# Seven block products in the first steps of three LSTMs, with their input sums made one LSTM earlier

## Chip, cores and metric

The kernel runs on one core of a Trainium2 chip. The metric is the device time of one execution in microseconds (us), the median of three executions. The core has a tensor engine for matrix products (PE; its weight loads are a queue of their own, PEld), a vector engine (DVE), a scalar engine for activation functions (ACT), GpSimd (POOL) and a queue, SP, that issues transfers.

## The reference

Four layers follow each other on x of 128 batches x 64 tokens x 256 channels: a two-matrix graph convolution with batch norms, a graph network with LSTMs, and two attention layers. Each normalises x over the channels, takes the positive part and adds its result to x. The change touches the second layer alone. It is, in the reference's words:

```
h = relu(einsum('ts,bsh->bth', adj, x @ Wg0 + bg0))
h = relu(einsum('ts,bsh->bth', adj, h @ Wg1 + bg1))
for p in range(1, 5):
    nw = Tv // p
    wins = h[:, :nw * p, :].reshape(Bv * nw, p, Hd)
    last = _lstm_last(Wih[p-1], Whh[p-1], bih[p-1], bhh[p-1], wins)
    idx = arange(nw) * p + (p - 1)
    h = h.at[:, idx, :].set(last.reshape(Bv, nw, Hd))

step(h, c):   g = x_t @ Wih.T + h @ Whh.T + bias;   i, f, gg, o = split(g, 4)
              c = sigmoid(f) * c + sigmoid(i) * tanh(gg);   h = sigmoid(o) * tanh(c)
```

So four LSTMs of one, two, three and four tokens run one after the other, each on what the one before has written. The states h and c are zero at the first step: that step needs only the products with Wih, of only three gates (i, g and o).

## The kernel before, in words

Everything is 32-bit float. The 8192 tokens lie in 16 chunks of 512 columns. The LSTM stage (about 274 to 1526 us of the profile) takes the chunks in eight pairs. A pair's tokens stand in one tile hT, channels on the partitions: two channel halves c (or k, as the operand of a product) of 1024 columns each, 64 tokens x 16 batches. For each pair the generator `lstms` (L1384) runs `single` (L1278, the one-token LSTM) and then `lstm` (L1026) for p = 2, 3 and 4. An LSTM of p tokens works on n = 512, 336 or 256 windows; m is half of n: 256, 168 or 128. `halves` splits the columns in two, j = 0 and 1.

All products of 256 x 256 by 256 x n that are not first steps, and all of `single`, are already done in seven block products of half the columns, in place of eight. `differences` (L309) makes four sums of the four operand blocks (t1 = b12 - b11, t3 = b22 - b12, t2 = b22 - t1, t4 = b21 - t2). A block product is called by its kind, 1 to 7: kinds 1, 2 and 3 take blocks b11, b21 and b22 as they are, kinds 5, 6, 7 and 4 take t1, t2, t3 and t4. `BLOCKS` (L1024) gives the index of each kind's weight block in a weight set, for Wih and Whh. Weight sets (one for each p and gate) are made in the first layer by `weight_sums` (L744), written to memory, and brought back into six buffers by `load_sets` (L883), two to four at a time, from the SP queue. A set has 15 blocks, 960 KB.

The first step of `lstm` before the change (L1107 to L1137) does not use block products: twelve whole products (three gates x two output halves x two operand halves, L1125) of n columns accumulate in six PSUM banks. Six of them need only operand half 0; a `yield` stands after these six. ACT then takes each bank through its activation (`first_acts`, L1112), DVE multiplies i by g (L1118), ACT takes tanh (L1119), DVE makes the state h (`new_state`, L1077) and, for the next step's products, its sums dh (L313 to L316). Behind the twelve products PE runs six block products of the next step that need no state (`A`, L1197), and then yields again. `operands_x` (L1086) makes the sums of the inputs of a later step, on POOL; the ones for step 1 stand at the beginning of `lstm`. For p = 3, where the number of windows is odd, three more POOL copies (L1097) bring blocks 1, 2 and 3 into contiguous columns.

Each later step (L1199 to L1256) does the same for the gates with both weights (class `Unit`): ACT copies two of the block products out of PSUM (L1160), DVE adds the others to them (L1163), ACT applies the activations (L1068).

The order is written out by hand: within this stage PE, DVE, ACT, POOL and SP each keep the order in which the program issues their instructions. Other work is put between: the loop at L1512 counts the `yield`s n of one pair, 0 to 21 (0 to 3 in `single`, 4 to 7 for p = 2, 8 to 13 for p = 3, 14 to 21 for p = 4), and at each one it issues the units that the lists at L1448 to L1456 name. They are parts of the convolutions of the next pairs (CONV and BEGUN, FIRST and BEGUN_FIRST in the first pair), the return of finished pairs (RESIDUAL) and the start of the next layer (AHEAD, LATE; FINAL in the last pair). Units that matter below, by number within `convolutions` (L980): unit 2 is `ln_stats` (DVE statistics L159, L160, then two POOL instructions for 1/sqrt, L99 and L100), unit 3 is a small DVE product that reads the POOL result (L194) and half of the normalisation on ACT (L196), unit 4 the other half, unit 5 an aggregation on PE (L214), unit 6 its two DVE copies (L1005), unit 7 a product (L915), unit 8 its lower bound on DVE (L921), unit 9 a product (L929), unit 10 its DVE add (L935). A unit of RESIDUAL adds transposed squares on DVE (L284).

PSUM has eight banks in this stage: two each with the tags x, y, z, and two for the units.

Of the kernel before, what the change touches and what calls it, by code (L numbers as in the profile page):

```python
# [13 lines left out]
P = 128  # L14
# [5 lines left out]
def kernel(  # L20
# [666 lines left out]
    with tc.manual_schedule(engines={mybir.EngineType.PE}):  # L687
# [56 lines left out]
        def weight_sums(p, q):  # L744
# [10 lines left out]
            far = dram.tile([P, 15, P], F32, tag=f"ws{p}{q}", name=f"wfar_{p}_{q}", bufs=1)  # L755
            nc.sync.dma_start(far[:, :9], w[:, :9])
            nc.sync.dma_start(far[:, 9:], w[:, 10:])
# [125 lines left out]
    def load_sets(n):  # L883
        for _ in range(min(n, len(coming))):
            p, q = coming.pop(0)
            wsets[p, q] = w1.tile([P, 15, P], F32, tag="wset", name=f"wset_{p}_{q}", bufs=6)
            nc.sync.dma_start(wsets[p, q], wfar[p, q])
# [136 lines left out]
    BLOCKS = {1: (0, 8), 2: (2, 9), 3: (7, 14), 4: (3, 10), 5: (4, 11), 6: (5, 12), 7: (6, 13)}  # L1024

    def lstm(p, hv, name, follows):  # L1026


        nb = hv.shape[3]
        nw = hv.shape[2] // p  # L1030
# [4 lines left out]
        inner = nb // 2 if odd else nb  # L1035
# [3 lines left out]

        def tokens(k, s, j):  # L1040
            v = hv[:, k, cols(s), :]
            if odd:
                return v[:, :, j * inner : (j + 1) * inner]
            return v[:, j * nw // 2 : (j + 1) * nw // 2, :]
# [41 lines left out]
        def operands_x(s):  # L1086

            t = l1.tile([P, 7 * (T // 3) * NB], F32, tag="xd", name=f"xd_{name}_{s}", bufs=2)
            t = [folded(t[:, i * m : (i + 1) * m]) for i in range(7 if odd else 4)]
            b = {(k, j): tokens(k, s, j) for k in range(KD) for j in range(2)}  # L1090
            for f in differences(nc.gpsimd, t[:4], b[0, 0], b[0, 1], b[1, 0], b[1, 1]):
                f()
            o = dict(zip((5, 6, 7, 4), t))
            for i, (kind, kj) in enumerate(((1, (0, 0)), (2, (1, 0)), (3, (1, 1)))):
                if odd:

                    nc.gpsimd.tensor_copy(t[4 + i], b[kj])  # L1097
                o[kind] = t[4 + i] if odd else b[kj]
            return o

# [4 lines left out]
        ox = {1: operands_x(1)}  # L1105

        banks = {(q, c): bank(f"g{q}_{name}_{c}", tag) for q, tag in ((0, "y"), (2, "z"), (3, "x"))  # L1107
                 for c in range(KD)}
        def first_acts(*qs):
            for q in qs:  # L1110
                for c in range(KD):
                    nc.scalar.activation(  # L1112
                        columns_of(gate(q, c)),
                        natural(banks[q, c][:, :n].rearrange("p (w b) -> p w b", b=nb)),
                        AF.Tanh if q == 2 else AF.Sigmoid, bias=bs[:, q * KD + c : q * KD + c + 1])
# [5 lines left out]
        products = [(q, c, k) for k in range(KD) for q in GATES[:3] for c in range(KD)]  # L1121
        for at, (q, c, k) in enumerate(products):
            if at == 6:
                yield
            nc.tensor.matmul(  # L1125
                banks[q, c][:, :n].rearrange("p (w b) -> p w b", b=nb), wsets[p, q][:, 2 * k + c, :],
                hv[:, k, : (nw - 1) * p + 1 : p, :], start=(k == 0), stop=(k == KD - 1))
        first_acts(0, 2)
        first_cell(0)
        first_acts(3)  # L1130
        first_cell(1)
        for c in range(KD):
            new_state(0, c, every)
            if not c:
                dh[0]()
# [63 lines left out]
        for s in range(1, p):  # L1199
            last = s == p - 1  # L1200
            B = [Unit(q, s) for q in (1, 3)]
            if not last:
                ox[s + 1] = operands_x(s + 1)
# [74 lines left out]
    def single(b, name, begun):  # L1278
# [57 lines left out]
        if begun:  # L1336
            for f in first + rest:
                f()
# [713 lines left out]
```

## Time and profile before

| | us |
|---|---|
| median of 3 executions | 1901.11 (1900.84 to 1902.15) |
| the profiled execution | 1899.42 |
| its span, first to last instruction | 1897.3 |
| PE busy | 1862.9 (98%) |
| DVE, ACT, POOL busy | 1238.9, 1015.9, 569.7 (65, 54, 30%) |
| LSTM stage from the first L1125, 293.5 to 1490 us: PE, DVE, ACT, POOL busy | 1180.9, 753.5, 652.8, 289.0 of 1196.5 |
| one pair of chunks, 611.0 to 768.5 us: PE, DVE, ACT, POOL busy | 155.9, 102.3, 86.8, 39.0 of 157.5 |

"Busy" is the time in which at least one instruction of the engine runs. PE records each 32-bit product as two instructions, so that the twelve products of a first step appear as 24. A group in the page's part 5 has its busy time, the mean duration of one, and the idle time of the engine just before it with what ended it. Matmuls overlap: the distance between the starts of two is shorter than the duration of one. In the timeline, each line has a start, a duration, the engine, the line of the program, what is written from what, and in brackets the idle time before it.

The pairs of chunks 2 to 7 run alike: from the first L1125 of p = 2 to the first product with a state, each takes 17.61 us; for p = 3 it is 11.49 to 11.64 us, and for p = 4 9.97 us. The first pair takes 16.99, 12.87 and 10.06 us, the last one 13.33, 9.68 and 9.01 us.

### The profile page before, as it was taken

The page shows a single profiled execution, that of the slowest core. Times are in us where ns is not written, and L with a number is a line of the kernel's source. Part 1 is how long each engine was busy: PE and PEld are TensorE (multiplying, and loading weights), DVE is VectorE, ACT ScalarE, POOL GpSimd, SP SyncE. Part 2 cuts the span into 40 slices and gives each one's busy share as a digit, 9 for nine tenths or more (in the row PEclk, how much of TensorE's full clock was granted, in tenths as well). Part 3 has the DMA queues.
Part 4 walks back from the last instruction along what each step waited for, and adds up shares of the span by engine and source line. Part 5 has one row for each costly group of instructions (what it writes and reads, how often), then busy time and mean ns, then how long its engine had stood idle before and what let it go on. Part 6 is the DMA issues. An engine that isn't in the chain of part 4 may idle for free.

```text
span 1897.3 us, 39092 instructions
## 1 busy us (share of the span) xinstructions
PE 1862.9 (98%) x15077; PEld 1478.2 (78%) x15077; DVE 1238.9 (65%) x3150; ACT 1015.9 (54%) x2284; POOL 569.7 (30%) x752
## 2 busy tenths in 40 slices
PE   8999989999999999999999999999999999999998
PEld 6877856895896798689589679868969967777776
DVE  6768746566576666667657666665565567677776
ACT  5766544556456446555645645655565544444453
POOL 5856621212221322222322231222122213233232
PEclk9999999999999999999999999999999999999999
DMA  3223643225334433333433443333144345444433
GB/s 114 78 68 149 232 168 109 72 88 184 106 129 145 144 128 129 113 119 115 150 117 129 150 139 137 130 109 106 54 150 139 103 134 157 135 139 152 143 114 113
DMA packets 111273, 241.45 MB, mean 127 GB/s; under 512 B 11504, under 2 KB 74864, under 8 KB 111088
## 3 DMA queue, kind: packets, MB, share of 16 engines
q1 hardware_dynamic: 110192, 237.09, 37.1%
q8 instruction: 119, 1.95, 0.4%
q0 software_dynamic: 320, 1.05, 0.2%
q10 hardware_dynamic: 576, 0.82, 0.1%
q14 instruction: 66, 0.54, 0.1%
HBM read 170.50 MB, written 68.42 MB: 126 GB/s over the span
## 4 chain that ended last, share of the span: by engine, by line
PE 86%; DVE 7%; POOL 3%; ACT 2%; issue 1%; DMA 0%; DVEq 0%; SPq 0%; ACTq 0%
PE x L1154 22%; PE z L1154 11%; PE g L1125 7%; PE v L1542 6%; PE y L1154 5%; PE x L1308 4%; PE y L1308 3%; PE p_q L1549 3%; PE v L915 3%; PE X L1738 3%; PE X L423 2%; PE X L499 2%; PE u L929 2%; PE Y L1738 1%; PE Y L423 1%
## 5 line engine op out<-in xcount | busy, mean ns | idle before, releaser
L1163 DVE TENSOR_TENSOR gates<-gates,x 128x128 f32<-128x128 f32 (+2 forms) x384 | 118.3, 320 | 332.1 <-PE x L1154 324.9
L1154 PE MATMUL x<-xd,wset 128*128 128x128 f32 (+2 forms) x1280 | 285.6, 311 | 0.7 <-DVE gates L1163 0.2
L1154 PE MATMUL x<-hd,wset 128*128 128x128 f32 (+2 forms) x1152 | 246.7, 303 | 0.0
L1212 POOL TENSOR_TENSOR gates<-gates 128x512 f32<-128x512 f32 (+2 forms) x48 | 74.9, 1560 | 521.7 <-ACT gates L1068 521.7
L1154 PEld LDWEIGHTS x<-xd,wset 128*128 128x128 f32 x1280 | 202.1, 190 | 19.1 <-DVE gates L1163 6.1
L1068 ACT ACTIVATE gates<-gates,bias 128x256 f32<-128x256 f32 (+4 forms) x384 | 170.4, 490 | 56.2 <-DVE gates L1163 52.8
L1154 PEld LDWEIGHTS x<-hd,wset 128*128 128x128 f32 x1152 | 185.1, 191 | 5.0
L1125 PE MATMUL g<-hT,wset 128*128 128x256 f32 (+2 forms) x576 | 183.9, 474 | 1.1 <-DVE hT L1079 1.1
L1160 ACT COPY gates<-y 128x128 f32<-128x128 f32 (+2 forms) x192 | 54.2, 293 | 212.9 <-PE y L1154 212.4
L1125 PEld LDWEIGHTS g<-hT,wset 128*128 128x128 f32 x576 | 108.6, 190 | 69.7 <-issue 38.5
L1154 PE MATMUL z<-hs,wset 128*128 128x128 f32 (+2 forms) x768 | 154.0, 303 | 0.0
L1154 PEld LDWEIGHTS z<-hs,wset 128*128 128x128 f32 x768 | 119.8, 191 | 3.3
L1160 ACT COPY gates<-x 128x128 f32<-128x128 f32 (+2 forms) x192 | 56.4, 295 | 93.7 <-PE x L1154 92.9
L1163 DVE TENSOR_TENSOR gates<-gates,z 128x128 f32<-128x128 f32 (+2 forms) x384 | 104.3, 315 | 0.1
L1068 ACT ACTIVATE gates<-x,bias 128x128 f32<-128x128 f32 (+2 forms) x192 | 74.7, 389 | 49.4 <-PE x L1154 46.5
L1154 PE MATMUL z<-hT,wset 128*128 128x128 f32 (+1 forms) x512 | 97.1, 302 | 0.0
L1112 ACT ACTIVATE gates<-g,bias 128x512 f32<-128x512 f32 (+2 forms) x144 | 74.5, 559 | 32.1 <-PE g L1125 31.6
L1154 PE MATMUL x<-hs,wset 128*128 128x128 f32 (+2 forms) x384 | 84.8, 303 | 0.0
L1223 ACT ACTIVATE gates<-cell 128x256 f32<-128x256 f32 (+2 forms) x144 | 55.2, 384 | 50.5 <-DVE cell L1222 49.0
L1154 PE MATMUL y<-xd,wset 128*128 128x128 f32 (+2 forms) x384 | 77.4, 304 | 3.4 <-ACT gates L1112 3.4
L1154 PE MATMUL y<-hd,wset 128*128 128x128 f32 (+2 forms) x384 | 80.1, 311 | 0.0
L1154 PEld LDWEIGHTS z<-hT,wset 128*128 128x128 f32 x512 | 76.7, 191 | 3.9 <-ACT gates L1112 0.6
(329 smaller groups left out, 4211.5 us busy)
## 6 DMA issues: line engine op xcount, KB each, us to landing
wset<-wfar SPq DMA_DIRECT2D x96, 960.0 KB, 6.6
hT<-far_h SPq DMA_DIRECT2D x124, 128.0 KB, 3.1
far_h<-hm SPq DMA_DIRECT2D x16, 512.0 KB, 3.0
far_n<-xs SPq DMA_DIRECT2D x16, 512.0 KB, 3.3
xs<-far_n SPq DMA_DIRECT2D x64, 128.0 KB, 4.2
far_x<-xs SPq DMA_DIRECT2D x16, 512.0 KB, 3.0
x<-far_x SPq DMA_DIRECT2D x64, 128.0 KB, 3.2
xt<-in_x_dram SPq DMA_DIRECT2D x15, 512.0 KB, 4.1
```

Of the source, the lines that this page charges most:

```text
L423: nc.tensor.matmul(self.banks[tag][:, i * CH // 2 : (i + 1) * CH // 2], w, self.at[kind], start=first and not i, stop=True, skip_group_che ...
L915: nc.tensor.matmul(banks[m], wg0_sb[:, k, m * P : (m + 1) * P], agg[:, k, :], start=(k == 0), stop=(k == KD - 1))
L1068: nc.scalar.activation(gate(q, c, part), src, AF.Tanh if q == 2 else AF.Sigmoid, bias=bs[:, q * KD + c : q * KD + c + 1])
L1112: nc.scalar.activation(columns_of(gate(q, c)), natural(banks[q, c][:, :n].rearrange("p (w b) -> p w b", b=nb)), AF.Tanh if q == 2 else AF. ...
L1125: nc.tensor.matmul(banks[q, c][:, :n].rearrange("p (w b) -> p w b", b=nb), wsets[p, q][:, 2 * k + c, :], hv[:, k, : (nw - 1) * p + 1 : p, ...
L1154: nc.tensor.matmul(folded(self.psum(kind)), wsets[p, self.q][:, BLOCKS[kind][i], :], (ox[self.s] if part == "x" else oh)[kind], start=firs ...
L1160: nc.scalar.copy(gate(self.q, kind // 5, halves[kind // 5]), self.psum(kind))
L1163: nc.vector.tensor_add(gate(self.q, *dst), gate(self.q, *a), self.psum(kind))
L1212: nc.gpsimd.tensor_mul(gates[:, 0, :, :n], gates[:, 0, :, :n], gates[:, 2, :, :n])
L1308: nc.tensor.matmul(folded(ps(g, kind)), wih1[:, g, KINDS1[kind], :], right[kind], start=kind in (2, 5, 1), stop=True, skip_group_check=True)
L1542: nc.tensor.matmul(ps[:, i, :], hT[:, k, j, :], w[:, k, first : first + D], start=(k == 0), stop=(k == KD - 1))
L1738: nc.tensor.matmul(st[c, tag][:, i * CH // 2 : (i + 1) * CH // 2].rearrange("p (a n) -> p a n", n=P), w, st[c, "o7"][kind], start=first an ...
```

## The change

1. The first step of p = 2, 3 and 4 is done in seven block products for each of the three gates (class `First`): 21 products of m columns in place of 12 of n. ACT copies kinds 1 and 5 of each gate, the `yield` follows, then kinds 3, 2, 6, 7 and 4 with DVE adds for 2, 6, 3 and 7, activations and cell products in between. Kinds 1, 6, 7 and 4 of a gate accumulate in the same columns of one bank.
2. `operands_x` is called by a new function `ending` at the end of the preceding LSTM, for steps 0 and 1: eight POOL sums there in place of four at the beginning of `lstm`. For p = 3 the three copies are gone, and the products read the strided blocks. The same is done for the sums of `single` (`block_sums`), which move ahead of the last `yield` of the p = 4 LSTM. The buffers for the sums are three of 1024 columns in place of two of 1176.
3. The weight sets have 14 blocks, 896 KB: block 1 was used by the old first step alone. Each set is written to memory in three transfers in place of two.
4. Three units move one `yield` later: CONV unit 4 of the second chunk (4 to 5), BEGUN unit 2 of the first (14 to 15), AHEAD unit 5 of the first (15 to 16). The six products of `A` stand in the order of kinds 3, 2, 5, before 5, 3, 2.

The diff, cut to its core:

```diff
@@ weight_sums
-            far = dram.tile([P, 15, P], F32, tag=f"ws{p}{q}", name=f"wfar_{p}_{q}", bufs=1)
-            nc.sync.dma_start(far[:, :9], w[:, :9])
-            nc.sync.dma_start(far[:, 9:], w[:, 10:])
+            far = dram.tile([P, 14, P], F32, tag=f"ws{p}{q}", name=f"wfar_{p}_{q}", bufs=1)
+            for at, n, src in ((0, 1, 0), (1, 7, 2), (8, 6, 10)):
+                nc.sync.dma_start(far[:, at : at + n], w[:, src : src + n])
@@ load_sets
-            wsets[p, q] = w1.tile([P, 15, P], F32, tag="wset", name=f"wset_{p}_{q}", bufs=6)
+            wsets[p, q] = w1.tile([P, 14, P], F32, tag="wset", name=f"wset_{p}_{q}", bufs=6)
@@ before lstm
+    def operands_x(p, hv, name, s):
+        nw, nb, inner, tokens = columns_x(p, hv)
+        m = nw * nb // 2
+        t = l1.tile([P, 2 * CH], F32, tag="xd", name=f"xd_{name}_{s}", bufs=3)
+        t = [t[:, i * m : (i + 1) * m].rearrange("p (a b) -> p a b", b=inner) for i in range(4)]
+        b = {(k, j): tokens(k, s, j) for k in range(KD) for j in range(2)}
+        for f in differences(nc.gpsimd, t, b[0, 0], b[0, 1], b[1, 0], b[1, 1]):
+            f()
+        return {5: t[0], 6: t[1], 7: t[2], 4: t[3], 1: b[0, 0], 2: b[1, 0], 3: b[1, 1]}
@@ lstm
-        ox = {1: operands_x(1)}
-        products = [(q, c, k) for k in range(KD) for q in GATES[:3] for c in range(KD)]
-        for at, (q, c, k) in enumerate(products):
-            if at == 6:
-                yield
-            nc.tensor.matmul(
-                banks[q, c][:, :n].rearrange("p (w b) -> p w b", b=nb), wsets[p, q][:, 2 * k + c, :],
-                hv[:, k, : (nw - 1) * p + 1 : p, :], start=(k == 0), stop=(k == KD - 1))
-        first_acts(0, 2)
+        class First:
+            def __init__(self, q, tags):
+                self.q, self.ps = q, [bank(f"{t}{q}_{name}_{i}", t) for i, t in enumerate(tags)]
+            def psum(self, kind):
+                return self.ps[kind in (2, 3)][:, m:n] if kind in (5, 3) else self.ps[kind in (2, 3)][:, :m]
+            def product(self, kind):
+                nc.tensor.matmul(folded(self.psum(kind)), wsets[p, self.q][:, BLOCKS[kind][0], :], ox[0][kind],
+                                 start=kind in (1, 3), stop=True, skip_group_check=True)
+            def copy(self, c, j, kind):
+                nc.scalar.copy(gate(self.q, c, halves[j]), self.psum(kind))
+            def add(self, dst, a, kind):
+                nc.vector.tensor_add(gate(self.q, dst[0], halves[dst[1]]),
+                                     gate(self.q, a[0], halves[a[1]]), self.psum(kind))
+        firsts = [First(q, tags) for q, tags in ((0, "yz"), (2, "yz"), (3, "xx"))]
+        all_first(1, lambda u: u.copy(0, 0, 1))
+        all_first(5, lambda u: u.copy(1, 1, 5))
+        yield
+        all_first(3)
+        all_first(2, lambda u: u.add((0, 0), (0, 0), 2))
+        all_first(6, lambda u: u.add((0, 1), (1, 1), 6), lambda u: u.add((0, 1), (0, 1), 3),
+                  lambda u: act(u.q, 0, every, gate(u.q, 0)))
         first_cell(0)
-        first_acts(3)
+        all_first(7, lambda u: u.add((1, 1), (1, 1), 7), lambda u: act(u.q, 1, halves[1], gate(u.q, 1, halves[1])))
+        new_state(0, 0, every)
+        dh[0]()
+        all_first(4, lambda u: act(u.q, 1, halves[0], u.psum(4)))
         first_cell(1)
-        for c in range(KD):
-            new_state(0, c, every)
-            if not c:
-                dh[0]()
+        new_state(0, 1, every)
         dh[1]()
         dh[2]()
@@ lstm
-        each(A, pe(5, "x"), pe(3, "x"), pe(2, "x"))
+        each(A, pe(3, "x"), pe(2, "x"), pe(5, "x"))
...
             if last:
                 load_sets(2)
+                ending()
@@ lstms
+        def ending(p):
+            if p < SKIP:
+                operands[p + 1] = {s: operands_x(p + 1, hv, names[p + 1], s) for s in range(2)}
+            elif sc < NCH // SUP - 1:
+                nxt = hTs[sc + 1].rearrange("p k (t b) -> p k t b", t=T)
+                operands[1] = block_sums(blocks(sc + 1, nxt), f"{sc + 1}_1")
@@ places
-    CONV = (3, 4, 4, 5, 6, 7, 8, 9, 10, 10), (3, 4, 4, 11, 12, 13, 14, 15, 16, 17, 18, 20)
-    BEGUN = (11, 13, 14, 16), (17, 19)
+    CONV = (3, 4, 4, 5, 6, 7, 8, 9, 10, 10), (3, 4, 5, 11, 12, 13, 14, 15, 16, 17, 18, 20)
+    BEGUN = (11, 13, 15, 16), (17, 19)
-    AHEAD = (4, 5, 7, 12, 14, 15), (6, 7)
+    AHEAD = (4, 5, 7, 12, 14, 16), (6, 7)
```

`all_first(kind, *fs)` issues, for each of the three gates in turn, the product of that kind and then the functions fs. `single` ends with `ending()` ahead of its last `yield`, too.

## The prediction

> **What bounds the kernel now.** I read the page first. The tensor engine is busy for nearly the whole span, and the chain that ended last lies on it.
>
> ```profile
> PE 1862.9 (98%) x15077; PEld 1478.2 (78%) x15077; DVE 1238.9 (65%) x3150; ACT 1015.9 (54%) x2284; POOL 569.7 (30%) x752
> PE 86%; DVE 7%; POOL 3%; ACT 2%; issue 1%; DMA 0%; DVEq 0%; SPq 0%; ACTq 0%
> L1125 PE MATMUL g<-hT,wset 128*128 128x256 f32 (+2 forms) x576 | 183.9, 474 | 1.1 <-DVE hT L1079 1.1
> ```
>
> Only 34 us of the span are without PE work (1897.3 - 1862.9). So two things alone count: PE time removed, and waits added on PE. A wait on PE has no slack to vanish in. The view of PE's waits in the LSTM stage (293 to 1490 us) says what could be won besides:
>
> ```profile
> PE z L1154 <- POOL xd L1097: 9.5, 6, 1.7
> PE y L1154 <- ACT gates L1112: 3.4, 3, 2.3
> ```
>
> The first line is p = 3, where PE waits six times for the POOL copies of the strided blocks. Then the timeline around the first step of p = 2 in the third pair of chunks (pairs 2 to 7 repeat it):
>
> ```profile
> 613.21 0.71 DVE L1324 TENSOR_TENSOR hT<-hs,gates 128x512 f32<-128x512 f32 x1
> 613.88 1.08 ACT L196 ACTIVATE cv<-xs,nmr_b,rstd_b 128x256 f32<-128x256 f32 x2
> 614.08 0.69 DVE L1324 TENSOR_TENSOR hT<-cell,gates 128x512 f32<-128x512 f32 x1 [0.16 <-ACT gates L1321]
> ...
> 617.00 0.23 POOL L99 TENSOR_SCALAR rstd_b<-mv_b 128x4 f32<-128x4 f32 x1 [8.74 <-DVE mv_b L160]
> 617.31 1.04 POOL L100 TENSOR_TENSOR rstd_b<-rstd_b,mhalf 128x4 f32<-128x4 f32 x1
> ...
> 618.32 0.73 POOL L313 TENSOR_TENSOR xd<-hT 128x256 f32<-128x256 f32 x1
> 618.93 0.15 DVE L194 SCALAR_TENSOR_TENSOR nmr_b<-mv_b,rstd_b 128x4 f32<-128x4 f32 x1
> 619.00 1.82 DVE L284 TENSOR_TENSOR xs<-xs,hT 128x512 f32<-128x512 f32 x2
> 619.01 1.27 POOL L314 TENSOR_TENSOR xd<-hT 128x256 f32<-128x256 f32 x1
> ```
>
> The reader is to see the order on POOL: 1/sqrt for the convolution (L99, L100) first, then the sums; and that DVE reads rstd_b in L194, ahead of L284 and of everything behind it. Two lines, of p = 2 and p = 4, give the price of dense DVE adds from PSUM:
>
> ```profile
> 634.62 1.51 DVE L1163 TENSOR_TENSOR gates<-gates,z 128x256 f32<-128x256 f32 x4
> 714.18 0.87 DVE L1163 TENSOR_TENSOR gates<-gates,z 128x128 f32<-128x128 f32 x4
> ```
>
> (1.51 - 0.41) / 3, about 0.34 to 0.37 us from one to the next at 256 columns, 0.20 at 128; the like row at 168 gives 0.25.
>
> [...]an add takes 0.28 us at 128 columns, 0.42 at 256. [...]the same POOL sum takes 0.73 us alone and 1.27 beside L284. [...]here the clock is 0.999 and no wait in the stage passes 2.3 us[...].
>
> **The change part by part.** Prices per block product (two records by their start-to-start distance): 0.432 us at 256 columns, 0.286 at 168, 0.224 at 128; whole products 0.858, 0.566, 0.432 at 512, 336, 256.
>
> *Products.* 12 whole become 21 block products: p = 2, 10.30 to 9.07; p = 3, 6.79 to 6.01; p = 4, 5.18 to 4.70. Gain 2.49 us a pair, 19.9 in eight pairs, all on PE.
>
> *POOL copies of p = 3.* Gone with their PE waits: -9.5. Reading strided blocks costs PE nothing: the 8-column pieces of the first pair's `single` run at the same 0.429 us a record as contiguous ones.
>
> *New evacuation.* Each first step gains six ACT copies, three ACT activations, twelve DVE adds. What matters is that kinds 6, 7 and 4 share PSUM columns: 7 of a gate waits for the add of 6, 4 for the add of 7. The adds of 7 stand on DVE behind the cell product, which waits for two activations, which wait for the adds of 3. PE has only own products behind: A and the units' products queue behind kind 4. The first step was covered by 12 long products; now this chain is bare. An add and its dependent one are 0.45 apart at 256 (as L1221 to L1222), 0.36, 0.32; so a gate's pair takes 0.8, 0.61, 0.52 us.
>
> *POOL order.* At the end of `single`, eight sums go in front of L99 and L100, whose statistics are issued at yield 3. t3 needs the state that DVE finishes at 613.92. Seven sums then take at least 0.69 to 0.75 each, to 619.1; L99 and L100 end at 620.5 instead of 618.35. L194 at yield 4, L284 and all adds of the first step queue behind on DVE.
>
> *Walk, p = 2* (same clock). PE: kinds 1 and 5 to 613.8; L214 needs the ACT rows of 613.88, ends 615.5; kinds 3, 2, 6 to 619.4. DVE: L194 at 620.5, L284 to about 622.1 (1.3 to 1.8 us); three adds of kind 2 to 623.1; first add of 6 done 623.5, so kind 7 starts at 623.7: PE idle 4.3 us. Second gate's pair done 624.8; activation (0.72) 625.55; cell product (0.69) 626.2; add of 7 626.65; three kinds 4 to 628.0; A, six products of 0.432, to 630.6. Before, A ended at 625.38. **+5.2.** L915 (3.4 us) hides the state behind A, as before.
>
> *p = 3.* PE from 653.85: kinds 1, 5, 3, 2, 6 to 658.1. DVE is busy to 658.5 with the statistics and L935 of yields 7 and 8. Adds of 2 to 659.25; second pair 660.55; activation (0.575) 661.2; cell 661.7; add 662.05; kinds 4 to 663.0; A to 664.7, against 664.25, which includes 1.55 of the POOL wait. **+0.45.**
>
> *p = 4.* PE from 701.05: to 704.4. DVE is busy to 704.3 with L284 and L921. Adds of 2 to 704.9; second pair 706.05; activation 706.6; cell 707.0; add 707.3; kinds 4 to 708.1; A to 709.4, against 707.55. **+1.9.** Moving BEGUN's statistics from yield 14 to 15 keeps 2.1 us of DVE out of this; that is in the walk.
>
> *First and last pair.* First: statistics and L194 straddle the first steps of p = 2 and p = 3 (L194 at 303.4 and 342.3 by the same count): +2.3, +3.5, and +1.75 for p = 4: +7.5. Last: no convolutions, so the bare chain, 1.8 us a step (worked out under the rivals), 5.4, less the 2.49 of the products and a wait of 1.6 us that p = 4 has now (9.01 us against 7.4 of products and fillers): +1.3, with L284 at yield 4 about +2 (0 to 3).
>
> *Rest.* Moved units: unit 4 at yield 5 runs on ACT beside L915; AHEAD's transposes (1.4 us of DVE) at yield 16 lie beside the products of kinds 6; nothing, at most 0.5 us a pair if DVE is late there. Sums at the end of p = 4 and `single`: same POOL work, earlier, nothing. Weight sets: 96 loads 64 KB smaller, no PE wait on a transfer in the view: nothing; one more SP transfer for each of 12 sets in the first layer, where PE waits for none: nothing.
>
> Sum: 6 × 7.6 + 7.5 + 2 = 55. On the profiled execution's 1899.4 (span 1897.3 plus 2.1) 1954.4; the median shown is 1.7 higher: **1956 us**.
>
> **Rivals.** *The adds keep up (faster).* Mechanism: twelve adds of 0.34 us fit beside fifteen products of 0.432. Price: -19.9 - 9.5, 1872 us. It decides if the 24 first steps wait less than (19.9 + 9.5) / 24 = 1.2 us each. DVE's 65% speaks for it; against it, even with DVE free, at 256 columns the first pair of adds begins 3.23 us after kind 3 (seven products and 0.21 to land), the second ends at 4.9, and activation, cell and add (0.72, 0.69, 0.42) let kind 4 start at 6.9, where products alone need 12 × 0.432 = 5.2: about 1.8 us, and the same count gives 1.8 at the other sizes. *The POOL queue is harmless.* If the rstd wait hides, p = 2 costs +1.6 instead of 5.2: six times 4.0, plus about 4 and 2: +30, 1931 us. Against it: the program order leaves L194 no other place. *The clock falls.* [...]1966 to 1978.
>
> **How the numbers follow.** A measurement tells about 0.2%, 3.8 us, from no change. Forecast (1942 to 1966) 0.60; POOL harmless 0.20; clock 0.12; adds keep up 0.05; gain and waits cancel within 0.2% 0.03. The unknown costs are the DVE start of the adds (±0.5 us in p = 2, p = 3 and p = 4: ±10) and the two middle rivals; range 1932 to 1976. Faster 0.05, same 0.03, slower 0.92.
>
> **What would show it.** In the profile after: the block products' PE time 158 against 178 us of start-to-start time; no wait for L1097; PE waits for DVE adds ahead of kinds 7 and 4, some 6 us for p = 2 of each middle pair, 3 for p = 3, 2 for p = 4; L99 behind eight sums at about 619 on the third pair's clock and L194 late with it; time from first product to first state product 22.8, 12.0 and 11.9 us instead of 17.61, 11.50 and 9.97. The prediction is wrong if kind 7 starts right behind kind 6, or if later waits on PE, which I found none of, take up the delay.

## The result and the profile after

| us | before | after |
|---|---|---|
| median of 4 executions | 1901.21 (1900.84 to 1902.15) | 1977.18 (1976.35 to 1978.09) |
| profiled execution; its span | 1899.42; 1897.3 | 1978.09; 1976.3 |

The ratio is 1.0399 (interval 1.0381 to 1.0417): 76 us slower, where 55 were forecast, and just outside the range. The page of the changed kernel, part 1, the chain's shares, and the largest group of the new products:

```profile
PE 1888.3 (96%) x15509; PEld 1534.6 (78%) x15509; DVE 1315.3 (67%) x3438; ACT 1076.5 (54%) x2500; POOL 598.8 (30%) x800
...
PE 76%; DVE 13%; ACT 4%; POOL 4%; issue 2%; DMA 0%; SPq 0%; DVEq 0%; ACTq 0%
...
L1120 PE MATMUL y<-xd,wset 128*128 128x256 f32 (+2 forms) x384 | 93.4, 358 | 65.2 <-POOL xd L315 23.5
```

PE had 34 us of the span without work, now 88 (1976.3 - 1888.3). The share of DVE on the chain went from 7 to 13%. The view of PE's waits in the LSTM stage (us in total, how often, the longest in us):

```profile
PE y L1120 <- POOL xd L315: 23.5, 9, 3.2
PE y L1120 <- DVE gates L1127: 22.0, 25, 3.2
PE y L1120 <- ACT gates L1124: 17.5, 17, 2.1
```

The 9.5 us of waits for the POOL copies (L1097) are gone. Three new kinds of wait stand at the new products: the forecast had only the second, L1127, the DVE adds ahead of kinds 7 and 4. The other two stand ahead of kind 5 (but for two waits of the first, 1.7 us, ahead of kind 4). This table gives the time from the first product of a first step to the first product on its new state, "middle" being the mean of six pairs:

| us | before | forecast | after |
|---|---|---|---|
| p = 2: first, middle, last pair | 16.99, 17.61, 13.33 | 19.3, 22.8, - | 21.63, 23.45, 19.86 |
| p = 3 | 12.87, 11.52, 9.69 | 16.4, 12.0, - | 18.60, 12.68, 14.64 |
| p = 4 | 10.06, 9.97, 9.01 | 11.8, 11.9, - | 14.81, 11.81, 10.86 |

The six middle pairs lose 53.0 us (forecast 45.6), the first 15.1 (7.5), the last 13.3 (2): 81.5. All other stretches of the stage together give 2.0 us back, and the layers ahead of it and behind it 0.5, which leaves the 79.0 by which the span grew.

Before the change, PE ran the first six products of p = 2 (twelve records) in the third pair without a wait:

```profile
611.20 5.31 PE L1125 MATMUL g<-hT,wset 128*128 128x512 f32 x12
```

The timeline of the changed kernel there (chosen lines in order of time, as in all timelines below: start, duration, engine, line, and in brackets the idle time before it with what ended it):

```profile
634.11 1.03 PE L1120 MATMUL y<-hT,wset 128*128 128x256 f32 x4
634.97 0.65 PE L1120 MATMUL x<-hT,wset 128*128 128x256 f32 x2
...
636.99 1.19 DVE L1358 TENSOR_TENSOR hT<-cell,gates 128x512 f32<-128x512 f32 x1 [0.17 <-ACT gates L1355]
638.27 0.65 ACT L1124 COPY gates<-y 128x256 f32<-128x256 f32 x2 [0.40 <-DVE hT L1358]
638.78 2.05 PE L1120 MATMUL y<-xd,wset 128*128 128x256 f32 x4 [3.16 <-POOL xd L315]
...
641.61 1.38 PE L214 MATMUL agg_b<-adjt_bd,cv 64*64 64x64 f32 x64
642.72 1.04 POOL L100 TENSOR_TENSOR rstd_b<-rstd_b,mhalf 128x4 f32<-128x4 f32 x1
643.12 1.29 DVE L1005 COPY cv<-agg_b 128x512 f32<-128x512 f32 x2 [2.80 <-PE agg_b L214]
644.33 0.15 DVE L194 SCALAR_TENSOR_TENSOR nmr_b<-mv_b,rstd_b 128x4 f32<-128x4 f32 x1
644.39 1.28 DVE L284 TENSOR_TENSOR xs<-xs,hT 128x512 f32<-128x512 f32 x2
645.60 0.74 DVE L1127 TENSOR_TENSOR gates<-gates,z 128x256 f32<-128x256 f32 x2
647.06 1.49 PE L1120 MATMUL y<-xd,wset 128*128 128x256 f32 x4
650.20 1.10 PE L1120 MATMUL y<-xd,wset 128*128 128x256 f32 x4 [0.88 <-DVE gates L1127]
651.58 1.89 PE L1170 MATMUL z<-hT,wset 128*128 128x256 f32 x8
```

The three products of kind 1 end at 635.6. Kind 5 starts at 638.78, right behind ACT's first copy of kind 1, which ends at 638.64. Before the change six products (5.15 us from start to start) ran here, and the last state of the preceding LSTM (L1358; L1324 before) was ready 3.57 us after the first of them. The releaser that the wait names, L315, makes a sum that kind 5 does not read; it merely ended last. What holds kind 5 is that it shares a PSUM bank with kind 1, whose copy into the tile `gates` waits for L1358, the last reader of the preceding LSTM's `gates` (experiment 2 shows it). L100 ends at 643.76, about as late as forecast, but L194 is not held by it: L1005 ends at 644.4, because L214 stands on PE behind the late kind 5. Kind 7 then follows kind 6 without a wait.

So the trace offers three suspects at p = 2, which end within a us of each other: the late products, the queue on POOL, and what stands on DVE ahead of the adds.

### The profile page after: what moved, and what is told of

Its sections match the earlier page's. It is cut to its first block, busy times and chain, and to the rows that moved or that the text cites. A ratio compares the mean times of both kernels' runs of the same rounds, so it can differ in the third digit from the quotient of the medians.

```text
span 1976.3 us, 40712 instructions
## 1 busy us (share of the span) xinstructions
PE 1888.3 (96%) x15509; PEld 1534.6 (78%) x15509; DVE 1315.3 (67%) x3438; ACT 1076.5 (54%) x2500; POOL 598.8 (30%) x800
## 4 chain that ended last, share of the span: by engine, by line
PE 76%; DVE 13%; ACT 4%; POOL 4%; issue 2%; DMA 0%; SPq 0%; DVEq 0%; ACTq 0%
PE x L1170 21%; PE z L1170 11%; PE y L1170 6%; PE v L1581 5%; PE y L1342 3%; PE p_q L1588 3%; PE x L1342 3%; DVE gates L1127 3%; PE X L1777 2%; PE y L1120 2%; PE X L423 2%; PE X L499 2%; PE u L929 2%; PE v L915 2%; PE Y L1777 1%
## 5 line engine op out<-in xcount | busy, mean ns | idle before, releaser
L1084 ACT ACTIVATE gates<-gates,bias 128x256 f32<-128x256 f32 (+4 forms) x528 | 240.2, 497 | 95.5 <-DVE gates L1179 50.6
L1170 PE MATMUL x<-xd,wset 128*128 128x128 f32 (+2 forms) x1152 | 256.2, 311 | 0.8 <-DVE gates L1179 0.7
L1170 PEld LDWEIGHTS x<-xd,wset 128*128 128x128 f32 x1152 | 180.9, 190 | 18.3 <-DVE gates L1179 5.6
L1120 PE MATMUL y<-xd,wset 128*128 128x256 f32 (+2 forms) x384 | 93.4, 358 | 65.2 <-POOL xd L315 23.5
L1170 PE MATMUL z<-hT,wset 128*128 128x128 f32 (+2 forms) x768 | 148.3, 306 | 0.0
L1120 PEld LDWEIGHTS y<-xd,wset 128*128 128x128 f32 x384 | 61.5, 198 | 91.5 <-issue 61.6
L1170 PEld LDWEIGHTS z<-hT,wset 128*128 128x128 f32 x768 | 119.3, 194 | 3.3
L1084 ACT ACTIVATE gates<-x,bias 128x128 f32<-128x128 f32 (+2 forms) x216 | 84.5, 391 | 51.3 <-PE x L1170 48.3
L1170 PE MATMUL x<-hT,wset 128*128 128x128 f32 (+2 forms) x384 | 85.7, 305 | 0.2
L313 POOL TENSOR_TENSOR xd<-hT 128x128 f32<-128x128 f32 (+2 forms) x72 | 42.3, 588 | 125.0 <-DVE hT L1095 110.0
```

The lines of the kernel that those rows point to most:

```text
L1084: nc.scalar.activation(gate(q, c, part), src, AF.Tanh if q == 2 else AF.Sigmoid, bias=bs[:, q * KD + c : q * KD + c + 1])
L1120: nc.tensor.matmul(folded(self.psum(kind)), wsets[p, self.q][:, BLOCKS[kind][0], :], ox[0][kind], start=kind in (1, 3), stop=True, skip_gr ...
L1170: nc.tensor.matmul(folded(self.psum(kind)), wsets[p, self.q][:, BLOCKS[kind][i], :], (ox[self.s] if part == "x" else oh)[kind], start=firs ...
```

## Experiments

"Middle" below is again the six middle pairs, "first step" the time of the table.

**1. Part two of the change alone.** From the kernel before, sums at the end of the preceding LSTM, no POOL copies; first products, weight sets and places of the units as before. The six products of A keep the changed order 3, 2, 5.

```diff
-        ox = {1: operands_x(1)}
+                operands[p + 1] = {s: operands_x(p + 1, hv, names[p + 1], s) for s in range(1, 2)}
```

> The kernel before with only the second part of the change: the input sums of step 1 made at the end of the preceding LSTM, p = 3 reads its strided blocks without POOL copies, whole first-step products and sets of 15 blocks kept. Sums theory (part two pays by itself, the loss is all in the seven products): PE's 9.5 us of waits for the POOL copies go, 1891 to 1893. Queue rival (sums ahead of L99 and L100 on POOL already hurt): nothing gained or a few us lost, 1898 to 1906.

Measured: 1894.93, ratio 0.9964 (0.9952 to 0.9977). Part two is a gain, some 2 us less than expected. All the loss, and more than 76 us of it, comes with the seven products; the smaller sets and the three moved units come with them and were not run apart.

**2. Kind 5 in the other bank.**

```diff
-                return self.ps[kind in (2, 3)][:, m:n] if kind in (5, 3) else self.ps[kind in (2, 3)][:, :m]
+                return self.ps[kind in (5, 3)][:, m:n] if kind in (2, 3) else self.ps[kind in (5, 3)][:, :m]
```

> The changed kernel with kind 5 in the second PSUM bank of its gate and kind 2 in the first, so that kind 5 no longer waits for ACT's copy of kind 1 out of the bank. It waits for the first POOL sum as before. Bank theory (kind 5 waits for that copy, and the copy for the last state of the preceding LSTM, which still reads the gates tile): three products of kind 5 move into the gap, about 2.3 us at p = 2 where they also run at half rate now, 0.9 at p = 3, 0.3 at p = 4, eight times: about 28 us, so 1949 (1940 to 1960). POOL theory (kind 5 waits for POOL's sums, as the wait view names it): 1977, within 3. Clock theory: as POOL theory, 1975.

**3. The tile `gates` in two halves.**

```diff
-        gates = l1.tile([P, 4, KD, CH], F32, tag="gates", name=f"gates_{name}", bufs=1)
+        gates = [l1.tile([P, 4, CH], F32, tag=f"gates{c}", name=f"gates{c}_{name}", bufs=1) for c in range(KD)]
```

> The changed kernel with the gates tile cut into one tile for each channel half, so that the copies of kind 1 (first half) wait for the state of that half, which is done earlier, not for the last state. POOL's product of two gates is two instructions instead of one. Gates theory: of the 41 us that PE waits at L1120 with POOL L315 or the ACT gates copy named, 25 to 35 go, and the half-rate stretches at p = 2 with them: 1945 (1935 to 1955). POOL theory: 1977, or up to 5 more for the added POOL instructions.

**4. Step 1's sums later.**

```diff
-                operands[p + 1] = {s: operands_x(p + 1, hv, names[p + 1], s) for s in range(2)}
+                operands[p + 1] = {0: operands_x(p + 1, hv, names[p + 1], 0)}
...
         yield
+        ox[1] = operands_x(p, hv, name, 1)
```

> The changed kernel with the four sums of step 1 issued after the first filler of the new LSTM, not at the end of the preceding one: half as many sums ahead of L99 and L100 on POOL. Queue theory (the step of the forecast that put 4.3 us of PE idle time at p = 2 on it): 8 x 3 to 4 us go at p = 2, 1950. Gates theory: the queue counts only in the first pair, where L194 waited last for L100; 3 to 5 us go, 1973 (1970 to 1976).

Measured: 1980.63, 1973.34 and 1975.82 (ratios 1.0416, 1.0383, 1.0388; intervals 1.0401 to 1.0432, 1.0368 to 1.0399, 1.0358 to 1.0418). None of the three edits alone gave more than 4 us; the 28 and 32 us expected of experiments 2 and 3 were wrong. The third pair of experiment 2:

```profile
635.40 1.03 PE L1120 MATMUL z<-xd,wset 128*128 128x256 f32 x4
643.75 0.16 DVE L194 SCALAR_TENSOR_TENSOR nmr_b<-mv_b,rstd_b 128x4 f32<-128x4 f32 x1 [2.31 <-POOL rstd_b L100]
645.70 1.10 PE L1120 MATMUL y<-xd,wset 128*128 128x256 f32 x4 [3.38 <-DVE gates L1127]
```

Kind 5 now starts right behind kind 1, before L315 has even begun (637.52): the bank held it, not POOL's sums. But the time does not fall, since kind 2 now shares the first bank and kind 6 has to wait for its adds, which stand on DVE behind an L194 that now waits for L100. The waits at L1127 rose from 22.0 to 43.7. In experiment 3, kind 5 came only half a us earlier (4.16 us after the first product), because ACT's copies stand behind two other rows (L196); so this edit did not take the late products away. What takes over further on:

```profile
641.66 1.10 PE L1120 MATMUL y<-xd,wset 128*128 128x256 f32 x4 [2.64 <-ACT gates L1124]
...
646.15 1.04 POOL L100 TENSOR_TENSOR rstd_b<-rstd_b,mhalf 128x4 f32<-128x4 f32 x1
647.22 0.16 DVE L194 SCALAR_TENSOR_TENSOR nmr_b<-mv_b,rstd_b 128x4 f32<-128x4 f32 x1 [1.53 <-POOL rstd_b L100]
```

Now L194 does wait for L100, as the forecast had it; the POOL queue had been hidden by less than a us. In experiment 4, the middle pairs stayed at 23.4 to 24.4 us at p = 2, but p = 3 of the first pair went from 18.60 to 15.70. Its timeline, in the changed kernel:

```profile
347.88 0.49 DVE L194 SCALAR_TENSOR_TENSOR nmr_b<-mv_b,rstd_b 128x4 f32<-128x4 f32 x1 [1.87 <-POOL rstd_b L100]
349.38 1.16 PE L1120 MATMUL y<-xd,wset 128*128 128x168 f32 x4 [2.50 <-DVE gates L1127]
```

and with the later sums:

```profile
345.75 0.49 DVE L194 SCALAR_TENSOR_TENSOR nmr_b<-mv_b,rstd_b 128x4 f32<-128x4 f32 x1 [0.29 <-POOL rstd_b L100]
347.25 1.16 PE L1120 MATMUL y<-xd,wset 128*128 128x168 f32 x4 [0.91 <-DVE gates L1127]
```

The queue on POOL is real where it ends last, which is there: kind 7 comes 1.6 us sooner. The other 1.3 us come with a half-rate stretch, a time in which PE is granted half its clock: it lay behind kind 7 in the changed kernel's profile (granted clock 0.50 from 352.00 to 355.41 us; the first two gates' kind 4 took 1.30) and is missing in this one (0.81). The four executions of experiment 4 lie far apart, from 1968.42 us at a mean granted clock of 0.994 to 1981.33 at 0.985, so its median says little.

**5. Late products, in the kernel before.** Nothing of the change is in this kernel: only the order of its twelve products differs.

```diff
-        products = [(q, c, k) for k in range(KD) for q in GATES[:3] for c in range(KD)]
+        products = [(q, c, k) for q in GATES[:3] for k in range(KD) for c in range(KD)]
```

> The kernel before with its twelve first-step products in another order: the two of block row 0 of a gate, then its two of block row 1, gate by gate, so that two products and not six are ahead of the first that needs the last state of the preceding LSTM. No work is added or removed. Cover theory (what the seven products lost is the work that ran while that state was being made): the last state ends 3.57, 1.45 and 0.6 us after the first product in the middle pairs, 4.95, 2.7 and 2.1 in the last; two products last 1.72, 1.13 and 0.86; so about 2.4 us are lost in each middle pair, 6 in the last, 4 in the first: 24 us, 1925 (1916 to 1932). Rival (that state has room): 1902, within 2.

Measured: 1921.28, ratio 1.0106 (1.0090 to 1.0121), 19.9 us more with the same work. PE's waits in the stage have a new first line:

```profile
PE g L1125 <- DVE hT L1324: 15.6, 8, 3.1
PE z L1154 <- POOL xd L1097: 7.2, 6, 1.2
PE g L1125 <- DVE hT L1083: 5.1, 10, 1.4
```

L1324 and L1083 make the last states. First steps at p = 2: 16.99 in the first pair, 19.62 in the middle, 18.40 in the last, that is +0, +2.0 and +5.1. The cover theory holds: a product that needs nothing of the preceding LSTM's last state is worth its place ahead of it, and the change left three short ones there.

**6. Two and three of the edits together.** Halves of `gates` with the later sums:

> The changed kernel with the gates tile in two halves and the sums of step 1 behind the first filler; the banks as they were, so that kind 5 still waits for ACT's copy of kind 1, which stands on ACT behind two normalizing rows of the filler. Stacked theory: L194 no longer waits for L100, but kind 5 still for ACT: 1 to 1.5 us of 23.1 at p = 2, 2 to 3 in the first pair: 1962 (1956 to 1968). Chain theory: 1970 to 1976, no less than either edit alone.

and with the banks set so that kind 5 waits for no copy and kind 6 for no add of kind 2:

```diff
+                return self.ps[kind in (2, 5)][:, m:n] if kind in (2, 3) else self.ps[kind in (2, 5)][:, :m]
...
-                                 start=kind in (1, 3), stop=True, skip_group_check=True)
+                                 start=kind in (1, 5), stop=True, skip_group_check=True)
```

> The changed kernel with three edits: kinds 5 and 2 in the second bank and 3 in the first (kind 5 waits for no copy, and kind 6 for no add of kind 2), the gates tile in two halves, and the sums of step 1 behind the first filler. Stacked theory (the wait for the copy and the rstd behind eight sums end within half a us of each other at p = 2, so that removing one shows the other): now kind 7 starts 9.3 to 10 us after the first product at p = 2 instead of 12.95; with 1 us at p = 3 and 3 to 5 in the first pair about 30 to 38 go: 1943 (1936 to 1952). Chain theory (the evacuation of kinds 6, 7 and 4 sets the end whatever is ahead of it): 1968 to 1977.

Measured: 1967.11 (ratio 1.0345, 1.0328 to 1.0362), within its band, and 1974.44 (1.0385, 1.0370 to 1.0400), a clear miss. The number lies in the band of the chain theory, but the trace shows another cause. The timeline of the three edits, third pair, p = 2:

```profile
631.65 1.03 PE L1120 MATMUL z<-xd,wset 128*128 128x256 f32 x4
633.18 1.20 DVE L1360 TENSOR_TENSOR hT<-cell,gates 128x512 f32<-128x512 f32 x1 [0.16 <-ACT gates L1357]
...
636.43 1.27 DVE L1005 COPY cv<-agg_b 128x512 f32<-128x512 f32 x2
637.98 0.69 DVE L194 SCALAR_TENSOR_TENSOR nmr_b<-mv_b,rstd_b 128x4 f32<-128x4 f32 x1 [0.28 <-POOL rstd_b L100]
638.06 0.59 PE L1120 MATMUL x<-xd,wset 128*128 128x256 f32 x2
638.60 1.82 DVE L284 TENSOR_TENSOR xs<-xs,hT 128x512 f32<-128x512 f32 x2
640.34 0.74 DVE L1127 TENSOR_TENSOR gates<-gates,z 128x256 f32<-128x256 f32 x2
642.25 2.08 PE L1120 MATMUL y<-xd,wset 128*128 128x256 f32 x4 [3.59 <-DVE gates L1127]
```

Kinds 1, 5, 3, 2 and 6 now run without a hole, up to 638.65. But the first add starts at 640.34, behind 6 us of other work that stands on DVE after the last state: statistics, L1005, L194, L284. The whole wait is back in front of kind 7 (3.59), and at half rate (two of its weight loads take 0.50 us, 0.30 in experiment 7) kind 7 takes 2.08 instead of 1.49. Why the banks took back 7 of the 10 us that the two other edits gave is open: the profiled execution with two edits is one of 1974.05 us at a mean clock of 0.988, while the other three took 1966.83 to 1967.21 at 0.992 to 0.993.

**7. DVE's fillers out of the way as well.** On top of the three edits, L284 with its copies, and L194, one place later (in the last pair by the list FINAL, moved like AHEAD):

```diff
-    RESIDUAL = (0, 3, 4), (2, 5, 6)
+    RESIDUAL = (0, 3, 5), (2, 5, 6)
-    ... (3, 4, 5, 11, 12, 13, 14, 15, 16, 17, 18, 20)
+    ... (3, 5, 5, 11, 12, 13, 14, 15, 16, 17, 18, 20)
-    AHEAD = (4, 5, 7, 12, 14, 16), (6, 7)
+    AHEAD = (5, 6, 7, 12, 14, 16), (6, 7)
```

> The kernel of the three edits (banks, gates in halves, step 1 sums later) with two fillers of p = 2 moved one place later on DVE, behind the adds of the first step: the residual sum L284 with the copy out and in that follow it, and L194 of the next pair's normalizing. Backlog theory (with the products dense, the first add stands on DVE behind the preceding LSTM's last state plus statistics, L1005, L194 and L284, 6 us in all; kind 7 waits 3.6 us and the clock halves after it): adds start about 2.4 us earlier, and the half-rate stretch of kinds 7 and 4 (1.5 us) goes: 3 to 4 us at p = 2 in six middle pairs, less 1 or 2 where L284 and L194 now stand: 1956 (1946 to 1964). Cover or chain theory: 1972 to 1978.

Measured: 1953.67, ratio 1.0266 (1.0249 to 1.0283): 21 us under the three edits, as the backlog theory had it. Third pair, p = 2:

```profile
635.84 1.27 DVE L1005 COPY cv<-agg_b 128x512 f32<-128x512 f32 x2
...
637.02 0.74 DVE L1127 TENSOR_TENSOR gates<-gates,z 128x256 f32<-128x256 f32 x2
638.93 1.49 PE L1120 MATMUL y<-xd,wset 128*128 128x256 f32 x4 [0.87 <-DVE gates L1127]
```

The adds start behind L1005, kind 7 waits 0.87 and takes 1.49, the full rate, and the first step takes 19.32 in all six middle pairs (23.37 with the three edits alone) and 15.61 in the last (19.84). At p = 3 the six middle pairs lost 6.7 us again (13.53 on average, 12.42 before). In the last pair of the changed kernel L284 waited 3.54 us for a transfer (hT, L254) with the adds behind it.

**8. The fillers alone,** those of the first pair too, with banks, `gates` and sums as the change has them:

> The changed kernel with fillers alone moved behind the first step's adds on DVE: L284 and L194 at p = 2 as before, and in the first pair L194, L900 and L988; banks, gates tile and the sums as the change has them. Backlog theory with both ends (late products and DVE's fillers must both go): in the middle pairs L1005 waits for the late L214 and ends at the time at which L284 began, so only 0.8 to 1.2 us a pair; 4 us in the first pair, 2 in the last: 1964 (1958 to 1970). If DVE's backlog alone sets the end: 4 us in each pair, as with the dense products, 1945 to 1952.

Measured: 1973.74, ratio 1.0378 (1.0363 to 1.0394), outside both bands. The middle pairs gain 1.1 us at p = 2, as the theory with both ends had it; the last gains nothing and the first loses 1.0, which it had not (in the first, L214 now waits 2.1 us for ACT behind the moved L194). So at p = 2 late products and DVE's backlog run side by side: taking away what makes the products late (experiment 6) gave 3 us, the backlog alone 3, both together 24.

**9. The same at p = 3 and p = 4.** Statistics and L935 at p = 3, L284 and L921 at p = 4 moved behind the adds too, with the first pair's fillers of experiment 8:

> Banks, gates in halves, step 1 sums later, and the fillers on DVE moved behind the adds at all three sizes: statistics and L935 at p = 3, L284 and L921 at p = 4, the first pair's L194, L900 and L988 at p = 2, besides the two of the kernel of 1953.7. Backlog theory: kind 7 waits 1.7 and 1.0 us at p = 3 and 4 and the clock halves after it (0.8 and 1.0): up to 3.5 us in each of six pairs and 4 in the first go: 1933 (1926 to 1942). If these waits come back where the fillers now stand, or at kind 4: 1946 to 1954.

Measured: 1974.93, ratio 1.0384 (1.0367 to 1.0402): worse than 1953.67 and outside both bands. PE's waits tell why:

```profile
PE y L1120 <- DVE gates L1127: 20.4, 42, 2.5
PE agg_c L214 <- DVE cv L935: 14.3, 12, 2.1
PE u L929 <- DVE cv L921: 12.7, 6, 2.1
```

The waits at L1127 fall from 34.8 to 20.4, but L935 and L921 make the operands of PE's next fillers, and 27.0 us of waits come back there. At these sizes this move of the backlog gains nothing: the adds and PE's other work want the same DVE time. Other places were not tried.

**10. The cell product behind the adds of kind 7,** so that kind 4 no longer waits for it, in the changed kernel and on top of experiment 7 ("the last kernel" in the second text):

```diff
-        first_cell(0)
-        all_first(7, lambda u: u.add((1, 1), (1, 1), 7), lambda u: act(u.q, 1, halves[1], gate(u.q, 1, halves[1])))
+        all_first(7, lambda u: u.add((1, 1), (1, 1), 7))
+        first_cell(0)
+        for u in firsts:
+            act(u.q, 1, halves[1], gate(u.q, 1, halves[1]))
```

> The changed kernel with only the first cell product issued behind the adds of kind 7. It takes the term of the forecast that is the same in every walk (kind 4 behind the cell product, 0.7 to 0.9 us) out of all 24 first steps: 12 to 18 us less, 1962 (1958 to 1966), if that term is real and nothing else ends there; none, 1975 to 1978, if the state that comes later gives it back ahead of the first product on the new state.

> The last kernel with the first cell product issued behind the adds of kind 7, and its tanh with it, so that kind 4 no longer waits for an add that stands behind the cell product. Chain theory: PE waits 0.9 us less ahead of kind 4 in each of 24 first steps, and the first half of the state comes 0.8 us later, behind A: 15 to 20 us under the last kernel. Backlog theory: the wait is 0.4 to 0.9 us and goes where a filler stands behind A: 8 to 12 us under it.

Measured: 1978.68 (1.0398, 1.0382 to 1.0413) and 1953.17 (1.0265, 1.0250 to 1.0280): nothing in either. In the changed kernel the waits at L1127 fall from 22.0 to 8.3, but 9.5 us come back ahead of A, where products wait for ACT's activations. The term is real as a wait and worth nothing as time.

**11. The clock.** Dummy transposes between kinds 1 and 5:

```diff
         all_first(1, lambda u: u.copy(0, 0, 1))
+        if p < 4:
+            keep_busy({2: 24, 3: 8}[p], f"w{name}")
```

> The changed kernel with dummy transposes on TensorE between kinds 1 and 5 (24 at p = 2, 8 at p = 3), about 2.5 and 0.9 us of a wait that is there anyway, so that the wait no longer lets the clock fall. Clock theory (the thirteen half-rate stretches cost what the walk left out): 10 to 20 us go, 1960 to 1967. Wait theory (what runs slower there ends before the next wait does): 2 us or less, 1974 to 1977.

Measured: 1994.94 (1.0497, 1.0479 to 1.0515). At p = 3 the transposes waited for the units' PSUM banks (20.5 us for L935), so the total says nothing. At p = 2 the run does answer:

```profile
639.66 2.78 PE L151 MATMUL idle_w<-ident 128*128 128x128 f32 x24
642.47 0.65 ACT L1124 COPY gates<-y 128x256 f32<-128x256 f32 x2 [0.40 <-PE idle_w L151]
642.98 1.10 PE L1120 MATMUL y<-xd,wset 128*128 128x256 f32 x4 [0.54 <-POOL xd L315]
```

Kind 5 takes 1.10 instead of 2.05, and the first step 23.09 to 23.11 in every middle pair. In the changed kernel's profile kind 5 runs at half rate in the third, fifth and seventh pair, and they take 0.4, 1.4 and 0.4 more than here. In the other three it runs at full rate (1.10), the half-rate stretch begins only at its end (at 474.88, 805.97 and 1140.48 us), and they take the same 23.11. The last pair takes 0.7 less here. At p = 2 the clock is worth about 3 us, not the 10 to 20 of the clock theory.

**12. The best of part two.** Experiment 1 with A's products again in the order 5, 3, 2, and the same with p = 2's sums where they were; and experiment 1 with only the latter:

```diff
-        each(A, pe(3, "x"), pe(2, "x"), pe(5, "x"))
+        each(A, pe(5, "x"), pe(3, "x"), pe(2, "x"))
```

> The kernel before with the input sums of step 1 made earlier at every size, and unit A's products again in the order 5, 3, 2. With the order 3, 2, 5 the first step of p = 2 took 0.42 us more and PE waited 6.3 us in three places for ACT's rows out of bank z. Order theory: 5 us less than with 3, 2, 5, 1890 (1888 to 1892). If POOL's sums beside the last state cost it: 1893 to 1896.

> The same with the sums of p = 2 where the kernel before has them. Order theory: as the last kernel, or 1 us less for the first pair: 1889 (1887 to 1891). Queue theory: 2 to 4 us under the last kernel.

> The kernel before with the input sums made earlier for p = 3 and p = 4 alone; p = 2 keeps its sums behind L99 and L100. With the sums moved at every size the first step of p = 2 took 0.42 us more in the middle pairs and 2.75 more in the first: 5.3 us, the queue on POOL. So 5 us under that kernel: 1890 (1888 to 1892), under both kernels of the case. If the 5 us are the last state beside POOL's sums and not the queue, 1892 to 1895.

Measured: 1891.54 (0.9949, 0.9934 to 0.9964), 1891.09 (0.9947, 0.9932 to 0.9962) and 1893.67 (0.9954, 0.9939 to 0.9969). The order is what counted: with 3, 2, 5 the first step of p = 2 took 18.03 to 18.05 in the middle wherever the sums stood, with 5, 3, 2 it takes 17.61. The queue theory falls for the middle pairs; in the first pair the place of the sums makes 0.7 us with the one order and 0.3 with the other. These versions are 8 to 11 us faster than the kernel before, about half a per cent.

## Why the prediction was right in direction and low in size

Of the 26 us between the 55 of the forecast and the 81.5 that the first steps lose, 7 are in the six middle pairs, 8 in the first pair and 11 in the last.

*Part two, -9.5.* Right: with A's order kept it measures 10.3 us (1901.87 to 1891.54). With the first step of old, the order 3, 2, 5 costs some 3 of these, and the prediction gave that order no cost; whether it costs anything with the seven products was not run.

*Walk, p = 2, +5.2.* The step that failed is "kinds 1 and 5 to 613.8". It took from the program order that PE runs six products in a row, and did not ask which of their banks and tiles are free. Kind 5 came 4.7 us after the first product, not 1.3. The middle pairs came out only 0.6 us over the forecast (5.8 against 5.2) by coincidence: the late kind 5 delayed L214 and L1005 by about as much as the step had put on L100. Kind 7 was forecast 12.5 us after the first product and came at 12.95; from there to the end of A it was 6.9 and 7.1. "PE idle 4.3 us ahead of kind 7" stood 3.2 us ahead of kind 5 instead. Kind 7 right behind kind 6 was the prediction's own sign of being wrong, and the middle pairs show it; the idle time of PE ahead of kind 7 appeared when the products were made dense (3.59).

*Last pair, about +2 (0 to 3).* It was 13.3: the largest miss. The same step is missing from it, and weighs most there, since the last state comes 4.95 us after the first product at p = 2. The order of products alone costs 5.1 and 1.65 us there at p = 2 and 3 in the kernel before (experiment 5). With dense products p = 3 goes from 14.64 to 12.05; with L284 out of the way besides, p = 2 from 19.84 to 15.61.

*First pair, +7.5.* It was 15.1. At p = 2 the forecast put L194 at 303.4; it stands at 305.75 (0.7 of this is the later start of the step), behind L284, statistics, L900 and L988 and a wait of 0.6 for L100. At p = 3 the POOL queue takes 1.6 and the half-rate stretch behind it 1.3 (experiment 4), at p = 4 late products with another such stretch (0.50 from 396.37 to 399.78 us) 2.4 (experiment 6: 12.38). L194 behind the sums was named; the late products and the clock were not in this term, which came out at half.

*Walks, p = 3 and p = 4.* +1.16 and +1.84 against +0.45 and +1.9. For p = 3 one pair of six, with a half-rate stretch, makes 0.3 of the difference. Kind 5 waits here, too (1.2 and 0.3 us in a middle pair), which the walks left out.

*Rivals.* "The POOL queue is harmless" was true in the middle pairs of the changed kernel, and its price (1931) wrong, for something else ended there at the same time. "The clock falls" gave 1966 to 1978, which holds the result, but its price was the author's estimate, which nothing measured before the change showed, and the wait it was tied to, 4.3 us ahead of kind 7 in each middle pair, did not come. Twelve stretches at half rate (granted clock 0.50) lie in the stage of the profile, eleven of 3.41 us and one of 6.83. Set beside the same first step without one, they cost 2.8 us at p = 2 (experiment 11), 1.7 at p = 3 in the fifth pair (14.09 against 12.40) and 1.5 in the last (14.64 against 13.15 in experiment 11), 6 us together; with some 1.5 each for p = 3 and p = 4 of the first pair the estimate is 9. It holds for the profiled execution alone: the executions of experiment 4 differ by 13 us and by their clock. "The adds keep up" is out: against part two alone with A's order kept, the seven products, with the sets and places that came with them, lose 86 us (1977.2 - 1891.5) where their shorter work promised 19.9.

*What stays open.* Of these 86 us, 23.5 were got back (experiment 7). Against the first steps of experiment 12 (1891.54), those of experiment 7 still take 15 us more at p = 2, 29 at p = 3 and 21 at p = 4. In its trace PE waits 29 us ahead of kind 7, and from the start of kind 7 to the start of A the 24 first steps take an estimated 43 us more than six products each at the prediction's prices. How these divide between the paced chain of kinds 6, 7 and 4, the shared DVE time and the clock is not settled. At p = 2 dense products still take 19.32 against 17.61. A second `gates` buffer (another 16 KB of each partition), and transposes into a bank of their own (the kernel has its eight PSUM banks in use), were not tried.

## What to carry to other kernels

Before products are replaced, count what of them runs ahead of the latest operand: work that needs nothing of it is cover (its order alone cost 19.9 us in experiment 5), and when it is halved the wait for that operand comes into the open, unless something else ends later. Then ask of each new product which bank, tile and copy it waits for, not only which operand. Where two chains end within a us of each other, the total time of an experiment on one of them shows little; read in its trace which wait took over, and take both away before a theory is dropped.

## What was not expected of the hardware

In the changed kernel's profile the granted clock falls to 0.50 in stretches of 3.41 us, once 6.83, while the longest wait of PE in the stage is 3.2 us. In each of the six middle pairs one begins at p = 2, around the end of the wait ahead of kind 5 (3.16 to 3.18 us, with products on both sides of it): from 0.66 us before that end to 1.35 after it. In the third pair it lasts from 638.72 to 642.13 us. In the fifth pair's p = 3 the clock is at half rate from 1024.4 to 1027.8 us, and the first step had waited only 1.18 and 0.84 us before:

```profile
1017.47 0.81 PE L1120 MATMUL y<-xd,wset 128*128 128x168 f32 x4 [1.18 <-ACT gates L1124]
1023.86 0.92 PE L1120 MATMUL y<-xd,wset 128*128 128x168 f32 x4 [0.84 <-DVE gates L1127]
```

The other five middle pairs have the same waits at p = 3 (1.17 to 1.19 and 0.83 to 0.85 us) and no stretch. What starts one is not shown. Nor does each stretch cost the same. At p = 2, where it begins at the end of kind 5, the first step takes 23.11 us as without one; where kind 5 itself runs at half rate (2.05 against 1.10 us) it takes 0.4 more, and 1.4 in the fifth pair, where the stretch is the double one.

The last state of `single` takes 1.19 us on DVE instead of 0.69 where POOL's sum L314 runs beside it (in the third pair from 636.99 and 636.90 us). Before the change that was so in the last pair only; the earlier sums bring it about in seven of eight.
